# Cross attention on one core: which head VectorE scales in quads 8 to 15, one half of a layer norm a slot later, query copies moved, two weight sums swapped

## The chip, the core and the metric

The kernel runs on one core of one Trainium2 chip. The core has five engines with instruction queues of their own, each taken in order: TensorE (PE; its weight loads are listed as PEld), VectorE (DVE), ScalarE (ACT), GpSimd (POOL) and SyncE (SP), which issues the DMAs. The metric is the device time of one execution in microseconds. Before the change the median of three runs was 573.78 us (573.76 to 574.15).

## The reference

Eight batches of 256 tokens with 1024 features attend to 256 context vectors of the same batch. There are 32 heads of 32 features; the context serves as keys and as values without a projection. All is float32, and the mask is all ones.

```python
residual = hidden_states
x = (hidden_states - mu) * jax.lax.rsqrt(var + LN_EPS) * ln_gamma + ln_beta
Q = _split_heads(x @ Wq.T)
K = _split_heads(memory_keys)
V = _split_heads(memory_values)
scores = jnp.einsum('bhsd,bhtd->bhst', Q, K) * scale
probs = jax.nn.softmax(scores, axis=-1)
attn = jnp.einsum('bhst,bhtd->bhsd', probs, V)
out = attn.transpose(0, 2, 1, 3).reshape(B, S, HIDDEN) @ Wout.T
return residual + out
```

## The kernel before

**Quads and slots.** Four heads fill the 128 partitions, so a batch has 8 quads and the kernel 64, numbered 0 to 63; quads 8 to 15 are batch 1. The main loop (L934) has one slot for each n from 0 to 63. In slot n the kernel computes the scores of quad n + 1 (`scores`, L486), the weighted values of quad n - 2 (`values`, L633), some steps of the output projection of the batch before (`product_steps`, L717), query products for a batch to come (`make_q`, L345, or `query_product`, L447), and then the softmax of quad n + 1 (`softmax_parts`). The order of the calls is the order on each engine's queue; nothing reorders them. Both projections are done with seven block products in place of eight (Strassen's scheme in Winograd's form), from batch 2 on for the queries, so weights and operands have to be added and subtracted first; GpSimd does these sums.

**The softmax of one quad** goes head by head, j = 0 to 3, each head with 2 x 128 queries against 256 keys:
- `exps(j)`: VectorE adds the mask and takes the row minimum (L524), ScalarE takes the exponential and its row sum (L528).
- `normalize(j)`: VectorE takes the reciprocals of the sums, `rden` (L535), and an engine scales the head, two instructions of 128 x 256 (a pair, below). In quads 1 to 15 ScalarE scales head 3 (L538). The others are scaled by GpSimd (L543), except that in quads 10 to 15 VectorE scales head 2 (also L543).
- `blocks(j)`: VectorE transposes the head's 32 x 32 blocks (L549) into `pT`.
- `aside`: ScalarE copies half of that (L555) for two DMAs on SP's queue that move it between partitions.

The calls on quads 8 to 15 before the change run: `exps` 0, 1, 2, `normalize(0)`, `exps(3)`, hooks, `normalize(1)`, `blocks(0)`, hooks, `normalize(2)`, `normalize(3)`, `blocks(1)`, `aside(0)`, `blocks(2)`, query copies (quads above 8), `blocks(3)`, `aside(1)`. The hooks are evacuations of the output projection: `store` adds an accumulator in PSUM to the residual tile r on VectorE (L759) and sends it; `take` adds without sending (L755); `add_p1` adds a kept product to r on GpSimd (L750).

**Queries.** `copies` move query products from PSUM to the query tile `qa`: `copy_q` on ScalarE (L354), `copy_product` on ScalarE (L457) or VectorE (L468). In quads 0 to 8 they stand between `exps(3)` and `normalize(1)`; in later quads behind `blocks(2)`. A PSUM bank is free for TensorE's next product when its copy is done.

**The layer norm of a batch** is prepared slots ahead: loads, statistics on VectorE (L227, L230, L232), the power -1/2 on GpSimd (L235), then `ln_norm`: a small product on GpSimd (`shift`, L245) and one ScalarE instruction over a half of 128 x 1024 (L248). VectorE transposes its blocks (L316) and 16 DMAs move them (L332). For batch 2 the table has both halves' `ln_norm` in slot 3, the transpositions in slots 4 and 5, and the DMAs in slots 5 to 7. `ln_norm` is called in a slot after `softmax_parts`.

**Sums of weights.** `sum_wo` (L182) and `sum_wq` (L396) each write one chunk of 128 x 512 on GpSimd; a table gives the slot of each chunk. They are issued at the end of a slot, behind the sums of attention outputs (`sum_at`, L693), of x (`sum_x`, L435) and L235.

Of the kernel before, what the change touches and what calls it, by code (L numbers as in the profile page):

```python
# [59 lines left out]
def xattn_kernel(  # L60
# [10 lines left out]
    nc = tc.nc  # L71
# [4 lines left out]
    NQ = NC  # L76
    NH = P // HD
# [84 lines left out]
    B11, B21, B22, T1, T2, T3, T4 = range(7)  # L162
# [328 lines left out]
    def softmax(*args):  # L491
        for _ in softmax_parts(*args):
            pass

    tails = []
    BY_ACT = range(1, 2 * NQ)
    BY_DVE = range(NQ + 2, 2 * NQ)


    def softmax_parts(n, copies=(), ahead=(), between=(), hooks={}, fill=()):  # L500

        fill = list(fill)

        def fill_in():
            if fill:
                fill.pop(0)()  # L510

        pss = scs[n]
        pT = pTs[n] = ptp.tile([P, 2, NI, NH, NS, K], F32, tag="pT", name=f"pT_{n}")
        pc = asp.tile([P, NI, NH, NS, K], F32, tag="pc", name=f"pc_{n}")
        es, mns, dens = {}, {}, {}

        def exps(j, part=range(NS)):
            if 0 in part:
                es[j] = ep.tile([P, NS, T], F32, tag="e", name=f"e_{n}_{j}")
                mns[j] = sm.tile([P, NS], F32, tag="mn", name=f"mn_{n}_{j}")  # L520
                dens[j] = sm.tile([P, NS], F32, tag="den", name=f"den_{n}_{j}")
            e, mn, den = es[j], mns[j], dens[j]
            for s in part:
                nc.vector.tensor_tensor_reduce(  # L524
                    out=e[:, s, :], in0=pss[j][:, s, :], in1=mbs[n // NQ], scale=1.0,
                    scalar=NO_SCORE, op0=ALU.add, op1=ALU.min, accum_out=mn[:, s : s + 1],
                )
                nc.scalar.activation(  # L528
                    e[:, s, :], e[:, s, :], AF.Exp, bias=mn[:, s : s + 1], scale=-1.0,
                    accum_out=den[:, s : s + 1],  # L530
                )

        def normalize(j):
            rden = sm.tile([P, NS], F32, tag="rden", name=f"rden_{n}_{j}")
            nc.vector.reciprocal(rden, dens[j])  # L535
            for s in range(NS):
                if j == NH - 1 and n in BY_ACT:
                    nc.scalar.activation(  # L538
                        es[j][:, s, :], es[j][:, s, :], AF.Copy, scale=rden[:, s : s + 1]
                    )  # L540
                    continue
                engine = nc.vector if j == NH - 2 and n in BY_DVE else nc.gpsimd
                engine.tensor_scalar(  # L543
                    es[j][:, s, :], es[j][:, s, :], rden[:, s : s + 1], 1.0,
                    ALU.mult, ALU.mult,
                )

        def blocks(j):
            nc.vector.transpose(  # L549
                pT[:, :, :, j, :, :].rearrange("p a i s k -> p (a i) s k"),  # L550
                es[j].rearrange("p s (b t) -> p b s t", t=K),
            )

        def aside(j):
            nc.scalar.copy(pc[:, :, ts(j, 2)], pT[:, 1, :, ts(j, 2)])  # L555

        if n == 0:
            for j in range(NH - 1):
                exps(j, (0,))
            yield  # L560
            exps(NH - 1, (0,))
            fill_in()
            yield
            for j in range(NH):
                exps(j, (1,))
            normalize(0)
            fill_in()
        else:
            exps(0)
            while tails:  # L570
                tails.pop()()
            for done in list(pvs):
                copy_at(done)
            exps(1)
            for hook in hooks.get("soon", ()):
                hook()
            exps(2)
            normalize(0)
            exps(3)
        if n <= NQ:  # L580
            for copy in copies:
                copy()
        for hook in hooks.get(0, ()):
            hook()
        normalize(1)
        fill_in()
        blocks(0)
        for hook in hooks.get(1, ()):
            hook()
        normalize(2)  # L590
        fill_in()
        if n in BY_ACT:
            normalize(3)
        blocks(1)
        aside(0)
        if n not in BY_ACT:
            normalize(3)
        fill_in()
        blocks(2)
        while fill:  # L600
            fill_in()
        if n > NQ:
            for copy in copies:
                copy()

        def tail():
            blocks(3)
            aside(1)

            for r in range(2):  # L610
                nc.sync.dma_start(pT[ts(2 * r, K), 1], pT[ts(2 * r + 1, K), 0])
            for load in between:
                load()
            for r in range(2):
                nc.sync.dma_start(pT[ts(2 * r + 1, K), 0], pc[ts(2 * r, K)])

        for load in ahead:
            load()
        if n < NQ or n > N - NQ:
            tails.append(tail)  # L620
        else:
            tail()
        yield
# [16 lines left out]
    def copy_at(n):  # L640
        b, c = divmod(n, NQ)
        k, c = divmod(c, NK)
        if c == 0:
            ats[b, k] = atp.tile([P, NK, NS, NA, K], F32, tag="at", name=f"at_{b}_{k}")
        for r, pv in enumerate(pvs.pop(n)):
            nc.scalar.copy(  # L646
                ats[b, k][:, c, :, ts(r, 2), :], pv.rearrange("p a s k -> p s a k")
            )
# [148 lines left out]
    for n in range(N):  # L797
# [12 lines left out]
    loads, stats, norms, trans, moves, biases, masks = (  # L810
        {n: [] for n in range(N)} for _ in range(7)
    )
    for b in range(1, B):
        first = NQ * (b - 1) + 2
        if b == 1:
            when = dict(moves=())
        elif b == 2:
            when = dict(
                loads=(0, 1), stats=(2, 3), norms=(3, 3), trans=(4, 5),
                moves=tuple(5 + (i + 2) // 6 for i in range(16)),  # L820
            )
        else:
            when = dict(
                loads=(first - 12, first - 11) if b == SPLIT + 1 else (first - 13, first - 12),
                stats=(first - 10, first - 9) if b == SPLIT + 1 else (first - 11, first - 9),
                norms=(first - 8, first - 7), trans=(first - 7, first - 6),
                moves=tuple(first - 6 + (i + 2) // 6 for i in range(16)),
            )
        for table, key in (
            (loads, "loads"), (stats, "stats"), (norms, "norms"), (trans, "trans"),  # L830
        ):
            for i, n in enumerate(when.get(key, ())):
                assert n < first
                table[n].append((b, i))
        for n in range(N):
            part = [i for i, slot in enumerate(when["moves"]) if slot == n]
            if part:
                assert n < first - 1
                moves[n].append((b, part))
        biases[NQ * b - 2].append(b)  # L840
        if b % 2 == 0:
            masks[NQ * b - 7].append(b)
# [2 lines left out]
    sums = {n: [] for n in range(N)}  # L845
    for n, which, *chunks in (
        (0, T3, 0), (1, T3, 1), (2, T2, 0), (3, T2, 1), (4, T3, 2, 3), (5, T2, 2, 3),
        (6, T4, 0, 1), (9, T4, 2), (11, T4, 3),
    ):
        sums[n] += [partial(sum_wo, which, c) for c in chunks]  # L850
    for n, which, *chunks in (
        (6, "T1", 0), (7, "T1", 1, 2, 3), (8, "T2", 0, 1), (10, "T2", 2), (11, "T2", 3),
        (11, "T3", 0), (12, "T3", 1, 2), (13, "T3", 3), (13, "T4", 0), (14, "T4", 1, 2, 3),
    ):
        sums[n] += [partial(sum_wq, which, o) for o in chunks]
# [37 lines left out]
    for c in range(NC):  # L893
        copy_x0(1, c, nc.scalar if c < NC // 2 else nc.vector)
    first = softmax_parts(0, (partial(copy_q, 1), partial(copy_q, 2)), (), (), {}, [
        partial(ln_stats, 1, 0), partial(ln_stats, 1, 1),
        partial(ln_norm, 1, 0, nc.vector),
# [17 lines left out]
    for b in range(B - 1):  # L915
        done, ends = 0, b == B - 2
        for i, counts in enumerate(steps_of(b)):
            n = NQ * (b + 1) + i
# [238 lines left out]
```

## Time and profile before

| what | value |
|---|---|
| median of three runs | 573.78 us |
| the profiled execution | 573.95 us |
| its span, first to last instruction | 572.2 us |
| TensorE clock granted | 1.00 throughout |
| L543 on VectorE, quads 10 to 15 | 12 times, 10.1 us, one 0.34 to 1.46 us |
| L543 on GpSimd | 470 times, mean 0.478 us |
| L248 on ScalarE, batch 2 | 2 times, 2.37 us together |

Times in the profile are microseconds from the first instruction; lengths are of single instructions or, where a count stands behind "x", of a run of equal ones. An idle time in brackets is that of the engine just before the row, with the engine and the line whose end released it. Consecutive instructions of an engine overlap a little in their records (a transposition of 0.70 us is followed by the next after 0.61). Busy time of TensorE is modelled, so "busy" is not the same as "at its peak"; the lengths of equal slots tell more.

Slots 8 to 15, which hold the softmaxes of quads 9 to 16, lie between 81.78 us and 154.90 us of the span.

### The profile page before, as it was taken

The page shows a single profiled execution, that of the slowest core. Times are in us where ns is not written, and L with a number is a line of the kernel's source. Part 1 is how long each engine was busy: PE and PEld are TensorE (multiplying, and loading weights), DVE is VectorE, ACT ScalarE, POOL GpSimd, SP SyncE. Part 2 cuts the span into 40 slices and gives each one's busy share as a digit, 9 for nine tenths or more (in the row PEclk, how much of TensorE's full clock was granted, in tenths as well). Part 3 has the DMA queues.
Part 4 walks back from the last instruction along what each step waited for, and adds up shares of the span by engine and source line. Part 5 has one row for each costly group of instructions (what it writes and reads, how often), then busy time and mean ns, then how long its engine had stood idle before and what let it go on. Part 6 is the DMA issues. An engine that isn't in the chain of part 4 may idle for free.

```text
span 572.2 us, 20196 instructions
## 1 busy us (share of the span) xinstructions
PE 563.0 (98%) x7266; PEld 394.5 (69%) x7266; DVE 471.7 (82%) x1712; ACT 423.7 (74%) x1464; POOL 396.3 (69%) x640
## 2 busy tenths in 40 slices
PE   9999999899999999999999999999999999999997
PEld 8788786677567677677676677667766767755454
DVE  5889889899998888978888788988878768779823
ACT  4699998897678867688577867778767776869920
POOL 2788899798677674875568575677658667448780
PEclk9999999999999999999999999999999999999999
DMA  8966668754888666877788767986658865536751
GB/s 308 395 178 194 186 192 243 225 178 117 260 286 263 197 182 188 267 229 213 199 244 241 196 188 193 261 274 184 191 152 243 247 195 139 140 104 182 215 160 73
DMA packets 47219, 119.02 MB, mean 208 GB/s; under 512 B 8976, under 2 KB 9744, under 8 KB 47120
## 3 DMA queue, kind: packets, MB, share of 16 engines
q1 hardware_dynamic: 46976, 117.74, 69.0%
q8 instruction: 57, 0.93, 0.7%
q14 instruction: 42, 0.34, 0.2%
q10 hardware_dynamic: 144, 0.01, 0.0%
HBM read 66.33 MB, written 11.53 MB: 136 GB/s over the span
## 4 chain that ended last, share of the span: by engine, by line
PE 73%; DVE 8%; ACT 6%; POOL 6%; DMA 4%; issue 2%; SPq 0%; DVEq 0%; POOLq 0%; ACTq 0%
PE po_S L717 18%; PE pq_A L447 16%; PE pv L633 10%; PE po_A L717 9%; PE sc L486 9%; PE pq_S L447 6%; ACT e L528 4%; PE po_end L784 3%; DVE pT L549 2%; POOL e L543 2%; DVE e L524 2%; DMA x<-in_x_dram 2%; PE po_last L784 1%; DMA pT<-pT 1%; DVE e L543 1%
## 5 line engine op out<-in xcount | busy, mean ns | idle before, releaser
L543 POOL TENSOR_SCALAR e<-e,rden 128x256 f32<-128x256 f32 x470 | 216.8, 478 | 130.7 <-DVE rden L535 125.7
L528 ACT ACTIVATE e<-e,mn 128x256 f32<-128x256 f32 x512 | 254.0, 501 | 48.2 <-DVE mn L524 47.1
L549 DVE STREAM_TRANSPOSE pT<-e 128x512 f32<-128x512 f32 x256 | 179.0, 703 | 37.0 <-POOL e L543 28.6
L524 DVE CUSTOM_DVE_ANT_0 e<-sc,mb 128x256 f32<-128x256 f32 x512 | 185.2, 415 | 27.1 <-PE sc L486 26.8
L555 ACT COPY pc<-pT 128x512 f32<-128x512 f32 x128 | 78.9, 617 | 53.3 <-DVE pT L549 34.4
L528 ACT ACTIVATION_READ_ACCUMULATOR e<-e,mn 128x1 f32 x512 | 98.2, 192 | 0.0
L486 PEld LDWEIGHTS sc<-k,qa 32*128 32x128 f32 x1024 | 46.0, 184 | 43.5 <-issue 23.6
L486 PE MATMUL sc<-k,qa 32*128 32x256 f32 x1024 | 73.9, 401 | 1.0 <-DVE qa L468 0.9
L717 PE MATMUL po_S<-wo,at 128*128 128x512 f32 x152 | 74.4, 606 | 0.2 <-DVE r L759 0.2
L633 PE MATMUL pv<-pT,v 64*32 64x128 f32 x4096 | 74.1, 274 | 0.0
L633 PEld LDWEIGHTS pv<-pT,v 64*32 64x32 f32 x4096 | 57.0, 105 | 22.5 <-issue 12.8
L717 PE MATMUL po_A<-wo,at 128*128 128x512 f32 x128 | 59.4, 605 | 0.4 <-ACT qa L354 0.4
L345 PE MATMUL pq<-xnT,wq 128*128 128x256 f32 (+1 forms) x240 | 55.0, 383 | 0.6 <-ACT qa L354 0.6
L447 PEld LDWEIGHTS pq_A<-xnT,wq 128*128 128x128 f32 x416 | 48.5, 192 | 6.2 <-issue 5.3
L717 PE MATMUL po_S<-wo,s 128*128 128x512 f32 x104 | 50.3, 608 | 1.9 <-DVE r L759 1.8
L345 PEld LDWEIGHTS pq<-xnT,wq 128*128 128x128 f32 x240 | 44.6, 190 | 8.9 <-issue 1.5
L447 PE MATMUL pq_A<-xnT,wq 128*128 128x128 f32 x416 | 48.5, 275 | 0.0
L535 DVE RECIPROCAL rden<-den 128x2 f32<-128x2 f32 x256 | 38.1, 149 | 8.2 <-ACT e L528 7.1
L524 DVE DVE_READ_ACCUMULATOR2_ANT mn<- 128x1 f32 x512 | 42.2, 82 | 0.0
L717 PEld LDWEIGHTS po_A<-wo,at 128*128 128x128 f32 x128 | 22.9, 189 | 26.1 <-issue 24.5
L717 PEld LDWEIGHTS po_S<-wo,at 128*128 128x128 f32 x152 | 25.5, 190 | 19.9 <-issue 19.5
L646 ACT COPY at<-pv 128x128 f32<-128x128 f32 x128 | 26.1, 253 | 8.9 <-PE pv L633 8.9
(102 smaller groups left out, 676.1 us busy)
## 6 DMA issues: line engine op xcount, KB each, us to landing
v<-in_kv_dram SPq DMA_DIRECT2D x32, 512.0 KB, 4.3
pT<-pT SPq DMA_DIRECT2D x128, 128.0 KB, 2.6
pT<-pc SPq DMA_DIRECT2D x128, 128.0 KB, 4.2
ring<-kept_T SPq DMA_DIRECT2D x20, 512.0 KB, 5.1
k<-in_kv_dram SPq DMA_DIRECT2D x32, 256.0 KB, 3.6
x<-in_x_dram SPq DMA_DIRECT2D x15, 512.0 KB, 5.5
r<-in_x_dram SPq DMA_DIRECT2D x28, 256.0 KB, 5.1
out_dram<-r SPq DMA_DIRECT2D x28, 256.0 KB, 3.7
```

What stands on the lines that cost most here:

```text
L345: nc.tensor.matmul(pqs[n], wq[:, o, c, :], xnTs[b](c), start=(c == 0), stop=(c == NC - 1),)
L447: nc.tensor.matmul(pqs[b][:, o, :], w[:, c], x_[:, c], start=begins and o + c == 0, stop=c == NK - 1, skip_group_check=True,)
L486: nc.tensor.matmul(scs[n][j][:, s, :], qa[r, n % NQ, ts(s, P)], ks[n - n % 2][r, n % 2, :], start=True, stop=True,)
L524: nc.vector.tensor_tensor_reduce(out=e[:, s, :], in0=pss[j][:, s, :], in1=mbs[n // NQ], scale=1.0, scalar=NO_SCORE, op0=ALU.add, op1=ALU.m ...
L528: nc.scalar.activation(e[:, s, :], e[:, s, :], AF.Exp, bias=mn[:, s : s + 1], scale=-1.0, accum_out=den[:, s : s + 1],)
L535: nc.vector.reciprocal(rden, dens[j])
L543: engine.tensor_scalar(es[j][:, s, :], es[j][:, s, :], rden[:, s : s + 1], 1.0, ALU.mult, ALU.mult,)
L549: nc.vector.transpose(pT[:, :, :, j, :, :].rearrange("p a i s k -> p (a i) s k"), es[j].rearrange("p s (b t) -> p b s t", t=K),)
L555: nc.scalar.copy(pc[:, :, ts(j, 2)], pT[:, 1, :, ts(j, 2)])
L633: nc.tensor.matmul(pvs[n][r][j * HD : (j + 1) * HD], vs[n - n % 2][ts(r, 2 * K), i, ds(n % 2 * P + j * HD, HD)], pT[ts(r, 2 * K), :, i, j, ...
L646: nc.scalar.copy(ats[b, k][:, c, :, ts(r, 2), :], pv.rearrange("p a s k -> p s a k"))
L717: nc.tensor.matmul(po, operand(b, name)[:, c], wo[:, which, c], start=begins and c == 0, stop=c == NK - 1, skip_group_check=not begins,)
```

## The change

Four edits. In quads 8 to 15 (before: 10 to 15) VectorE scales head 1 (before: head 2), and GpSimd scales head 2; in these quads `normalize(2)` is called ahead of `blocks(0)`. Query copies of quad 9, whose softmax is in slot 8, stand between `exps(3)` and `normalize(1)`. The second half of batch 2's `ln_norm` is in slot 4. One chunk of `sum_wo` goes from slot 9 to slot 8, and one of `sum_wq` from slot 8 to slot 9.

```diff
-    BY_DVE = range(NQ + 2, 2 * NQ)
+    BY_DVE = range(NQ, 2 * NQ)
...
-                engine = nc.vector if j == NH - 2 and n in BY_DVE else nc.gpsimd
+                engine = nc.vector if j == 1 and n in BY_DVE else nc.gpsimd
...
-        if n <= NQ:
+        if n <= NQ + 1:
             for copy in copies:
                 copy()
         for hook in hooks.get(0, ()):
             hook()
         normalize(1)
         fill_in()
+        if n in BY_DVE:
+            normalize(2)
         blocks(0)
         for hook in hooks.get(1, ()):
             hook()
-        normalize(2)
+        if n not in BY_DVE:
+            normalize(2)
         fill_in()
...
-        if n > NQ:
+        if n > NQ + 1:
             for copy in copies:
                 copy()
...
-                loads=(0, 1), stats=(2, 3), norms=(3, 3), trans=(4, 5),
+                loads=(0, 1), stats=(2, 3), norms=(3, 4), trans=(4, 5),
...
-        (6, T4, 0, 1), (9, T4, 2), (11, T4, 3),
+        (6, T4, 0, 1), (8, T4, 2), (11, T4, 3),
...
-        (6, "T1", 0), (7, "T1", 1, 2, 3), (8, "T2", 0, 1), (10, "T2", 2), (11, "T2", 3),
+        (6, "T1", 0), (7, "T1", 1, 2, 3), (8, "T2", 0), (9, "T2", 1), (10, "T2", 2), (11, "T2", 3),
```

## The prediction

> **What bounds the kernel now.** I read the busy shares and the chain of waits first, then TensorE's timeline with its idle times, then the lengths of the loop's slots, then VectorE, GpSimd and ScalarE in the slots where TensorE stands still.
>
> ```profile
> PE 563.0 (98%) x7266; PEld 394.5 (69%) x7266; DVE 471.7 (82%) x1712; ACT 423.7 (74%) x1464; POOL 396.3 (69%) x640
> PE 73%; DVE 8%; ACT 6%; POOL 6%; DMA 4%; issue 2%; SPq 0%; DVEq 0%; POOLq 0%; ACTq 0%
> ```
>
> TensorE bounds the whole, but 27% of the chain is elsewhere. In order of time the chain is TensorE alone from 152.99 us on; before that it runs through the other engines. So only the start can pay. The TensorE timeline, start, length, and in brackets the idle time ahead:
>
> ```profile
> 61.36 2.83 PE L345 MATMUL pq<-xnT,wq 128*128 128x256 f32 x12 [0.63 <-ACT qa L354]
> 91.97 6.28 PE L717 MATMUL po_A<-wo,at 128*128 128x512 f32 x14 [0.41 <-ACT qa L354]
> 106.79 1.99 PE L717 MATMUL po_S<-wo,s 128*128 128x512 f32 x4 [1.75 <-DVE r L759]
> 138.00 3.81 PE L447 MATMUL pq_A<-sx,ring 128*128 128x128 f32 x32 [0.68 <-DVE qa L468]
> 146.36 0.71 PE L486 MATMUL sc<-k,qa 32*128 32x256 f32 x8 [0.95 <-DVE qa L468]
> 152.99 1.98 PE L717 MATMUL po_S<-wo,at 128*128 128x512 f32 x4 [0.18 <-DVE r L759]
> ```
>
> A slot (one value of n) begins with L486 on TensorE. Measured from one L486 to the next, slot 4 lasts 8.20 us (58.50 to 66.70) and slot 5, with the same work, 7.55. Slots 9 to 15 do what slots 17 to 23 do again without idle time: slot 9 lasts 8.84 against 8.37, slot 10 10.53 against 8.51, slots 11, 12 and 13 the same as their twins (9.37, 8.51, 8.51), slot 14 9.61 against 8.51, slot 15 10.20 against 8.51. The excess is 0.66, 0.47, 2.02, 1.10 and 1.69 us: 5.94 in all; behind 152.99 there is nothing to win.
>
> VectorE's scaling of the third head (L543) and GpSimd beside it:
>
> ```profile
> 96.69 2.73 DVE L543 TENSOR_SCALAR e<-e,rden 128x256 f32<-128x256 f32 x2
> 107.75 0.64 DVE L543 TENSOR_SCALAR e<-e,rden 128x256 f32<-128x256 f32 x2
> 116.09 0.63 DVE L543 TENSOR_SCALAR e<-e,rden 128x256 f32<-128x256 f32 x2
> 124.67 1.63 DVE L543 TENSOR_SCALAR e<-e,rden 128x256 f32<-128x256 f32 x2
> 133.33 2.67 DVE L543 TENSOR_SCALAR e<-e,rden 128x256 f32<-128x256 f32 x2
> 142.64 1.82 DVE L543 TENSOR_SCALAR e<-e,rden 128x256 f32<-128x256 f32 x2
> ...
> 94.94 1.83 POOL L543 TENSOR_SCALAR e<-e,rden 128x256 f32<-128x256 f32 x4
> 96.74 1.26 POOL L693 TENSOR_TENSOR s<-at,at 128x512 f32<-128x512 f32 x1
> ...
> 53.34 2.37 ACT L248 ACTIVATE x<-x,shift,rstd 128x1024 f32<-128x1024 f32 x2 [0.35 <-POOL shift L245]
> 60.39 0.82 ACT L354 ACTIVATE qa<-pq,qa 128x256 f32<-128x256 f32 x2
> ```
>
> One instruction, six times, 0.63 to 2.73 us for a pair. In quad 10 the first of the pair began at 96.69, GpSimd's sum L693 at 96.74, and both ended about together; so with the second and GpSimd's next sum. The short pairs met no large sum. The chain at that place:
>
> ```profile
> 100.64 2.30 issue
> 102.97 0.55 POOL rstd L235
> 103.52 1.25 POOL wo L182
> 104.78 1.23 POOL r L750
> ```
>
> GpSimd stands 2.3 us until VectorE, late by its scaling, delivers the variance (L232); then come L182 and L750, VectorE's store L759, and the 1.75 us of TensorE.
>
> **The change part by part.** Times are those of this execution; "lead" is how much earlier than before.
>
> **The norm a slot later.** ScalarE's two L248 take 1.14 each, at 53.34 to 55.62, ahead of quad 5's exponentials. Without the second, these start 1.14 earlier, and so do the query copies L354: done at 60.07, not 61.21. TensorE was ready for them at 60.66 (L633 from 59.57, 1.09 long): 0.66 won. The second L248 now stands behind slot 4's tail copy, which ended at 62.41, now 61.3; it ends at 62.45, before quad 6's exponentials began (62.69). Its shift (L245, 0.25) moves on GpSimd from slot 3 to slot 4, behind the scaling of head 2. That scaling started at 60.60 because of rden from ScalarE's exponentials; now about 59.3, so the sums behind start at 60.4, not 61.49: a GpSimd lead of 1.05. GpSimd is then the chain almost without a gap until 75.70, so VectorE and ScalarE keep about 1.05. The block transposition of that half (slot 5, at 65.73) and its DMAs on SP's queue stay behind the same instructions. Were that cover gone, the L248 would cost its 1.14.
>
> **Quads 8 and 9.** Two more scaling pairs on VectorE, one GpSimd pair (0.93) less each. A pair alone is 0.63; it now comes right behind rden of head 1, when GpSimd scales head 0. The row for that: at 142.64 the first of a pair took 0.55 against 0.35, beside a GpSimd scaling that began at 142.56. So 0.63 to 1.03 a pair; I take 0.85, the middle. Quad 8 hides it: VectorE stood 0.26 and 0.78 us there. Quad 9 does not (no idle time from 87.60 to 91.75): VectorE's lead falls to 0.2.
>
> The Trainium skill, page "SBUF — State Buffer", section "Who interferes with whom", speaks against this place: any GpSimd instruction holds the port pair shared with VectorE whole, and VectorE's two-port scaling then blocks fully. The sums above agree. By the rule each scaling could wait a GpSimd scaling's 0.48, a pair 1.6, and eight pairs would be up to 6 us dearer than by 0.85.
>
> **Query copies of slot 8.** Two L354 of 0.36 move in front of the fourth head's scaling and one tail copy. Ready with the exponentials (before 89.43, lead 1.05), they end at 89.1; TensorE is ready at 91.49 - 0.66 = 90.8, so 0.47 is won. The scaling behind them waits for rden until 89.4 anyway; without that it would be 0.7 later.
>
> **Quads 10 to 15.** The order does the work: GpSimd's second pair now waits for rden of head 2, which VectorE computes behind its own scaling. Between head 0 and head 2 GpSimd can start no sum. VectorE can meet a sum only when GpSimd is still at the slot before; then rden of head 2 and the transposition of head 0 queue behind the pair, and GpSimd's second pair waits for that rden.
>
> Slots 9 and 10: VectorE starts quad 10 at 91.5, scales at 94.6 to 95.5 beside head 0, transposes until 98.4 (before 101.23), delivers L232 at 99.95 (102.81). GpSimd: head 2 from 95.8, done 96.75; three sums of 1.25 to 100.6; rstd 0.55; one sum, then L750 until 103.6 (106.01). L759 ends 104.3. TensorE arrives there at 97.04 + 1.07 + 1.09 + 0.96 + 3.57 = 103.73: 0.62 us idle stay, 1.40 of 2.02 are won.
>
> Slots 11 to 13: TensorE full, lead 2.53, so slot 14 begins at 132.6. The others must hold it. ScalarE (8.25 us of work in slots 10 and 11) has a lead of 2.6 from VectorE's and keeps it. In quad 12 nothing changes. In quad 13 GpSimd ends its sums at 120.85, VectorE comes at 121.0 and pays about 1.0, not 1.63. In quad 14 VectorE comes at 128.85, GpSimd's last sum ends at 129.3: about 1.15 instead of 2.67. L468 ends at 132.95 (before 137.85); TensorE needs it at 134.8. GpSimd's last sum into the ring ends at 135.15, needed at 137.5. All 1.10 of slot 14 are won.
>
> Slots 14 and 15: quad 15's scores now come at 133.7 and hold VectorE. It scales at 137.3, waits for a sum until 137.65, L468 ends at 141.35; the second half of slot 15's scores is due at 141.08 + 0.54 = 141.6. Then mask bias, exponentials, L759 at 148.2; TensorE is there at 147.8. Of 1.69, 1.27 are won. GpSimd is the thin place: its sums take 6.25 us in slots 11 to 13, its scaling 1.85, and the hold about 0.9: 9.0 a slot against TensorE's 8.51, paid from the lead.
>
> **The swapped sums.** L182 and L396 take 1.25 each; slots 8 and 9 keep theirs. Their readers are products of slots 13 and 14. Nothing, within 0.05.
>
> Sum: 0.66 + 0.47 + 1.40 + 1.10 + 1.27 = 4.90. Span 572.2 - 4.9 = 567.3. The execution took 573.95, 1.75 around its span, and the median of three is 573.78: 573.78 - 4.9 = **568.9**. From slot 16 on TensorE has no idle time and the code is the same.
>
> **The rivals.**
> All idle time goes (0.62 and 0.42 too): 573.78 - 5.94 = 567.8. For it: these rests hang on L759 alone. Against: GpSimd's row of sums up to L750 has no gap to give.
> The scalings of quads 13 to 15 still meet sums, because GpSimd, held between its heads, falls behind: slots 14 and 15 keep their excess. 573.78 - 0.66 - 0.47 - 1.40 = 571.25. For it: 9.0 against 8.51. Against: the lead of 2.5.
> L750 comes no earlier: only ScalarE's two edits pay, 573.78 - 1.13 = 572.65. For it: the sums are as many as before. Against: the 2.3 us that GpSimd stood for L232.
> Slower: GpSimd falls behind for good. It decides from where GpSimd's last sum ends over 1.25 us after VectorE's rden of head 1; then every pair of quads 10 to 15 costs 2.7. 6 x 2.7 + 2 x 0.85 - 10.1 = 7.8 more for VectorE; less 1.45 idle in quad 12 and the 1.13 of ScalarE, 5.2: 579.0. For it: the hold. Against: GpSimd began head 0 late only in quad 10, by 0.12 us; in quad 12 it stood 1.94 before it, in quad 15 1.08.
> That the change doesn't do what it says is hardly one: the loop calls the scaling directly behind rden of head 1 in all eight quads, and VectorE takes its queue in order.
>
> **How the numbers follow.** The forecast (568.0 to 570.3, from the pair at 0.63 or 1.03 and one sum met in quad 14 or 15) 0.58; all idle gone 0.10; half of it 0.17; ScalarE alone 0.06; slower 0.09. A difference under 0.2%, 1.15 us, can't be told from none: the ScalarE case is at that bound and counts as same. Faster 0.85, same 0.06, slower 0.09. The range 567.7 to 571.6 holds the first three and leaves out 0.2.
>
> **What would show it.** VectorE's L543 sixteen times, mostly 0.34 to 0.6 us, not 0.95. TensorE's waits for L354 gone; at L759 in slot 10 0.6 instead of 1.75; at L468 none. GpSimd's L543 466 times, not 470, and GpSimd waiting for rden ahead of its second pair. Slot 16 begins near 150.0, not 154.9. Wrong would be: long pairs in quads 13 to 15, or a new wait of TensorE for the ring.

## The result, and the profile after

The changed kernel took 570.98 us (median, 570.41 to 571.32); the kernel before, beside it on the same chip, 573.94. The ratio is 0.9947 with a 95% interval of 0.993 to 0.9965: faster by 2.96 us, where 4.90 was forecast (568.9). The profiled execution took 571.32 us, its span 569.5. The added code has three lines, so L717, L750, L759, L693 and L633 of before are now L720, L753, L762, L696 and L636; kernels below that leave those lines out keep the old numbers. The medians below are over all executions; three far longer ones (637 us of e_copies, 1366 of a_late2 and 1979 of the kernel before) are left out of the ratios.

The page's busy shares and chain of waits of the changed kernel:

```profile
PE 561.8 (99%) x7266; PEld 393.9 (69%) x7266; DVE 468.5 (82%) x1716; ACT 423.7 (74%) x1464; POOL 394.0 (69%) x636
PE 80%; POOL 7%; DVE 5%; ACT 3%; issue 3%; DMA 1%; SPq 0%; DVEq 0%; POOLq 0%; ACTq 0%
```

TensorE's share of the chain rises from 73% to 80%, not to the whole: 20% is still elsewhere. TensorE's timeline shows where, with the only two rows between 56 and 160 us that have an idle time (in brackets):

```profile
105.56 1.98 PE L720 MATMUL po_S<-wo,s 128*128 128x512 f32 x4 [1.20 <-DVE r L762]
...
145.91 1.13 PE L720 MATMUL po_S<-wo,s 128*128 128x512 f32 x2 [1.31 <-POOL wo L182]
```

The waits for L354 in two slots, for L468, and the 0.18 us for the store in slot 15 are gone. The wait for the store in slot 10 is 1.20 us, not the 0.62 of the forecast. The second row is new: TensorE waits for a weight sum of GpSimd. Slot lengths, from one L486 to the next, in us (the slot from 58.50 us, which the prediction calls slot 4, is slot 5 by the count of the others; only slots that differ are shown):

| slot | before | after | without idle time |
|---|---|---|---|
| 5 | 8.20 | 7.55 | 7.55 |
| 9 | 8.84 | 8.36 | 8.37 |
| 10 | 10.53 | 9.98 | 8.51 |
| 14 | 9.61 | 8.51 | 8.51 |
| 15 | 10.20 | 9.89 | 8.51 |

Won: 0.65, 0.48, 0.55, 1.10 and 0.31, together 3.09. Left: 1.47 in slot 10 and 1.38 in slot 15.

VectorE's scaling L543 in the changed kernel, from VectorE's timeline, all eight quads:

```profile
81.12 0.62 DVE L543 TENSOR_SCALAR e<-e,rden 128x256 f32<-128x256 f32 x2
88.03 0.61 DVE L543 TENSOR_SCALAR e<-e,rden 128x256 f32<-128x256 f32 x2
95.84 1.04 DVE L543 TENSOR_SCALAR e<-e,rden 128x256 f32<-128x256 f32 x2
105.62 0.62 DVE L543 TENSOR_SCALAR e<-e,rden 128x256 f32<-128x256 f32 x2
113.72 0.62 DVE L543 TENSOR_SCALAR e<-e,rden 128x256 f32<-128x256 f32 x2
122.29 0.90 DVE L543 TENSOR_SCALAR e<-e,rden 128x256 f32<-128x256 f32 x2
130.09 1.09 DVE L543 TENSOR_SCALAR e<-e,rden 128x256 f32<-128x256 f32 x2
138.64 1.05 DVE L543 TENSOR_SCALAR e<-e,rden 128x256 f32<-128x256 f32 x2
```

Eight pairs take 6.55 us; the six of before took 10.12. None of them lasts as long as one that met a large sum before (1.63 to 2.73). What GpSimd does around a pair, for the one at 113.72 (heads 0 and 2 of its quad, no sum between them):

```profile
112.44 0.93 POOL L543 TENSOR_SCALAR e<-e,rden 128x256 f32<-128x256 f32 x2 [1.16 <-DVE rden L535]
114.73 0.93 POOL L543 TENSOR_SCALAR e<-e,rden 128x256 f32<-128x256 f32 x2 [1.35 <-DVE rden L535]
```

GpSimd's timeline has the three rows that the rest of the case turns on:

```profile
67.92 0.93 POOL L543 TENSOR_SCALAR e<-e,rden 128x256 f32<-128x256 f32 x2 [0.64 <-DVE rden L535]
...
91.53 0.55 POOL L235 TENSOR_TENSOR rstd<-ve,mhalf 128x1 f32<-128x1 f32 x1 [1.19 <-DVE ve L232]
...
144.58 1.28 POOL L182 TENSOR_TENSOR wo<-wo 128x512 f32<-128x512 f32 x1
```

In the first GpSimd stands for a reciprocal; in the second for the variance of slot 8; the third is the sum that TensorE waits for in slot 15. To compare executions I count from the L486 near 58.5 us (58.50 before, 58.92 after). GpSimd's L235 in slot 8 then comes at 32.20 us before and at 32.61 after: 0.41 later, though the norm edit was to bring it earlier. From there the chain runs through GpSimd's sums without a gap that could give, in the chain of waits of the changed kernel:

```profile
99.22 1.24 POOL sx L435
...
102.31 1.24 POOL wq L396
103.55 1.25 POOL r L753
104.82 0.70 DVE r L762
105.56 1.98 PE po_S L720 x4
```

### The profile page after: what moved, and what is told of

It is laid out like the page before. It is cut to its first block, busy times and chain, and to the rows that moved or that the text cites. A ratio compares the mean times of both kernels' runs of the same rounds, so it can differ in the third digit from the quotient of the medians.

```text
span 569.5 us, 20200 instructions
## 1 busy us (share of the span) xinstructions
PE 561.8 (99%) x7266; PEld 393.9 (69%) x7266; DVE 468.5 (82%) x1716; ACT 423.7 (74%) x1464; POOL 394.0 (69%) x636
## 4 chain that ended last, share of the span: by engine, by line
PE 80%; POOL 7%; DVE 5%; ACT 3%; issue 3%; DMA 1%; SPq 0%; DVEq 0%; POOLq 0%; ACTq 0%
PE po_S L720 20%; PE pq_A L447 18%; PE pv L636 10%; PE sc L486 10%; PE po_A L720 10%; PE pq_S L447 7%; PE po_end L787 3%; ACT e L528 2%; POOL e L543 2%; DVE e L524 2%; DVE pT L549 1%; PE po_last L787 1%; POOL wq L396 1%; POOL wo L182 1%; DMA pT<-pT 1%
## 5 line engine op out<-in xcount | busy, mean ns | idle before, releaser
L543 POOL TENSOR_SCALAR e<-e,rden 128x256 f32<-128x256 f32 x466 | 215.3, 478 | 128.7 <-DVE rden L535 126.1
L549 DVE STREAM_TRANSPOSE pT<-e 128x512 f32<-128x512 f32 x256 | 179.0, 704 | 35.6 <-POOL e L543 26.2
L486 PEld LDWEIGHTS sc<-k,qa 32*128 32x128 f32 x1024 | 46.2, 184 | 42.1 <-issue 20.1
L720 PE MATMUL po_S<-wo,at 128*128 128x512 f32 x152 | 74.3, 606 | 0.0
L636 PE MATMUL pv<-pT,v 64*32 64x128 f32 x4096 | 74.1, 274 | 0.0
L486 PE MATMUL sc<-k,qa 32*128 32x256 f32 x1024 | 73.6, 401 | 0.1
L636 PEld LDWEIGHTS pv<-pT,v 64*32 64x32 f32 x4096 | 57.0, 105 | 22.5 <-issue 12.4
L720 PE MATMUL po_A<-wo,at 128*128 128x512 f32 x128 | 59.4, 605 | 0.0
L720 PE MATMUL po_S<-wo,s 128*128 128x512 f32 x104 | 50.2, 607 | 2.5 <-POOL wo L182 1.3
L720 PEld LDWEIGHTS po_A<-wo,at 128*128 128x128 f32 x128 | 23.0, 190 | 25.6 <-issue 24.4
L720 PEld LDWEIGHTS po_S<-wo,at 128*128 128x128 f32 x152 | 25.5, 190 | 19.5 <-issue 19.5
L753 POOL TENSOR_TENSOR r<-r,p 128x512 f32<-128x512 f32 x24 | 30.6, 1275 | 5.0 <-DMA r<-in_x_dram 4.0
```

The source lines that it names most:

```text
L486: nc.tensor.matmul(scs[n][j][:, s, :], qa[r, n % NQ, ts(s, P)], ks[n - n % 2][r, n % 2, :], start=True, stop=True,)
L543: engine.tensor_scalar(es[j][:, s, :], es[j][:, s, :], rden[:, s : s + 1], 1.0, ALU.mult, ALU.mult,)
L549: nc.vector.transpose(pT[:, :, :, j, :, :].rearrange("p a i s k -> p (a i) s k"), es[j].rearrange("p s (b t) -> p b s t", t=K),)
L636: nc.tensor.matmul(pvs[n][r][j * HD : (j + 1) * HD], vs[n - n % 2][ts(r, 2 * K), i, ds(n % 2 * P + j * HD, HD)], pT[ts(r, 2 * K), :, i, j, ...
L720: nc.tensor.matmul(po, operand(b, name)[:, c], wo[:, which, c], start=begins and c == 0, stop=c == NK - 1, skip_group_check=not begins,)
L753: nc.gpsimd.tensor_tensor(r, r, p1s[b], ALU.add)
```

## The experiments

Two sets: parts of the change alone on the kernel before, and then single mends or reversals on the changed kernel. Times are medians; each ratio is to the kernel before, run beside it on the same chip. Beside these kernels the kernel before took 575.08, 574.83 and 574.60 us in the mean of each set of runs, and 573.95 beside the changed kernel, in part because some of its executions had a lower TensorE clock (last section). So for the same time the ratios here come out up to 0.002 lower than the first one, and what decides below are the traces.

**The two ScalarE edits, each alone.**

```diff
 e_norm:
-                loads=(0, 1), stats=(2, 3), norms=(3, 3), trans=(4, 5),
+                loads=(0, 1), stats=(2, 3), norms=(3, 4), trans=(4, 5),
 e_copies:
-        if n <= NQ:
+        if n <= NQ + 1:
...
-        if n > NQ:
+        if n > NQ + 1:
```

> The kernel before with the norm edit alone. Theory: ScalarE's edit wins TensorE 0.66 us in slot 4, but slot 10's wait for L759 ends when GpSimd and VectorE get there, and their lead fell to about 0.2 us by slot 6 in the changed kernel; the 0.66 turns up as a longer wait in slot 10, so the time is 0.0 to 0.3 us shorter (573.5 to 573.9). Rival (the sum on record): the terms add, 0.66 us shorter (573.2).

> The kernel before with slot 8's query copies moved, alone. Theory: slot 9 loses its 0.47 us of idle time and slot 10's wait grows by as much: no change, 573.7 to 574.0. Rival: the terms add, 0.47 us shorter (573.4).

Measured: the norm edit 574.12 us, ratio 0.999 (0.9973 to 1.0007); the copies 574.88, ratio 1.0001 (0.9987 to 1.0014). Neither is told from no change. The waits of TensorE that grew, first with the norm edit, then with the copies:

```profile
92.26 6.28 PE L717 MATMUL po_A<-wo,at 128*128 128x512 f32 x14 [0.93 <-ACT qa L354]
```

```profile
106.77 3.36 PE L717 MATMUL po_S<-wo,s 128*128 128x512 f32 x4 [2.29 <-DVE r L759]
```

The norm edit takes 0.67 out of slot 5 (7.53 us) and slot 9's wait grows from 0.41 to 0.93; what TensorE won it stands later, most of it already in slot 9 and not, as expected, in slot 10. The copies take 0.47 out of slot 9 and the wait in slot 10 grows from 1.75 to 2.29, by 0.54. In both, the later wait ends at a time that the edit hardly moves: 33.31 us after the L486 near 58.5 against 33.47 before, and 48.36 against 48.29. With the copies alone the four products behind the wait also took 3.36 us, not 1.99 (last section), and slot 14 lasted 8.86 us, not 9.61.

**The scaling alone**, in all eight quads, and in the six that VectorE had before.

```diff
 both:
-                engine = nc.vector if j == NH - 2 and n in BY_DVE else nc.gpsimd
+                engine = nc.vector if j == 1 and n in BY_DVE else nc.gpsimd
...
+        if n in BY_DVE:
+            normalize(2)
         blocks(0)
...
-        normalize(2)
+        if n not in BY_DVE:
+            normalize(2)
 e_scale only:
-    BY_DVE = range(NQ + 2, 2 * NQ)
+    BY_DVE = range(NQ, 2 * NQ)
```

> The kernel before with the scaling edit alone (head 1 on VectorE in quads 8 to 15, the second reciprocal and GpSimd's pair ahead of the first transposition). Theory: it alone sets when L759 ends in slot 10 and when GpSimd ends its sums in slot 14, so it wins nearly all that the whole change wins: 570.9 to 571.3, with slot 4's and slot 9's idle times back and slot 10's wait shorter by about as much. Rival: the terms add, so 1.1 us of the gain is missing: 572.1.

> As the run before, but only in quads 10 to 15. Theory: without the pair of quad 9 VectorE delivers the variance (L232) of slot 8 0.6 to 0.7 us earlier, GpSimd starts its row of sums up to L750 as much earlier, and both of TensorE's remaining waits (L759 in slot 10, the sum L182 in slot 15) are 0.6 us shorter: 570.2 to 570.7. Rival: the two quads relieve GpSimd of a pair each, and without that it is later: 571.5 to 572.5. Second rival: they don't matter, the same as the run before.

Measured: 571.18 us, ratio 0.9936 (0.9919 to 0.9953), and 570.80, ratio 0.9925 (0.9907 to 0.9944). The scaling edit alone gives what the whole change gives, and its two added quads give nothing. The theory for six quads failed in its mechanism: slot 10 has no wait in either kernel; the wait that is shorter without the two quads is slot 9's (0.41 against 1.03), and slot 15's goes only from 1.35 to 1.24. TensorE's waits with the scaling in all eight quads:

```profile
61.54 5.42 PE L345 MATMUL pq<-xnT,wq 128*128 128x256 f32 x24 [0.64 <-ACT qa L354]
...
92.77 6.28 PE L720 MATMUL po_A<-wo,at 128*128 128x512 f32 x14 [1.03 <-ACT qa L354]
...
145.95 1.12 PE L720 MATMUL po_S<-wo,s 128*128 128x512 f32 x2 [1.35 <-POOL wo L182]
```

Here the two waits for ScalarE stand, and the wait in slot 10 isn't there at all. In the changed kernel it is the other way round. The store in slot 10 (L759, now L762) starts 47.54 us after the mark before, 46.16 with the scaling alone, 45.90 after: the scaling moves it by 1.4, the ScalarE edits by 0.26. What these win ahead of it, TensorE loses again at it.

**Which head.** The whole change, but VectorE scales the third head as before.

```diff
-                engine = nc.vector if j == 1 and n in BY_DVE else nc.gpsimd
+                engine = nc.vector if j == NH - 2 and n in BY_DVE else nc.gpsimd
...
-        if n in BY_DVE:
-            normalize(2)
         blocks(0)
...
-        if n not in BY_DVE:
-            normalize(2)
+        normalize(2)
```

> The changed kernel with VectorE scaling head 2 again, in the old order of calls, but still in quads 8 to 15; the other three edits stay. Theory: VectorE meets GpSimd's sums again (a pair 1.6 to 2.7 us in most quads) and the gain is gone: 573.0 to 575.5. Rival: the gain comes from relieving GpSimd of two pairs and from ScalarE's edits, not from which head it is: 571 to 572.

Measured: 577.97 us, ratio 1.0053 (1.0034 to 1.0073), slower than I had expected. Two of its pairs on VectorE, and what TensorE waits for:

```profile
81.81 2.74 DVE L543 TENSOR_SCALAR e<-e,rden 128x256 f32<-128x256 f32 x2
...
99.10 2.73 DVE L543 TENSOR_SCALAR e<-e,rden 128x256 f32<-128x256 f32 x2
```

```profile
109.18 3.47 PE L717 MATMUL po_S<-wo,s 128*128 128x512 f32 x4 [3.60 <-DVE r L759]
```

Quad 8's pair now meets GpSimd's three sums into the tile `ring` (L396, one run of 3.83 us from 81.85) and the variance of slot 8 is late by that; GpSimd stands 2.51 us for it; quad 10's pair meets sums as before the change. So the gain needs the head or the order of calls that goes with it, both of which this run puts back, and with the third head and the old order more quads on VectorE are a loss. Part of the loss is a lower clock behind the stop of 3.60 us (last section).

**Short pairs, or an early reciprocal?** In the changed kernel VectorE computes head 2's reciprocal ahead of the transposition of head 0. This run puts the call behind it and leaves the head that VectorE scales.

```diff
-        if n in BY_DVE:
-            normalize(2)
         blocks(0)
         for hook in hooks.get(1, ()):
             hook()
-        if n not in BY_DVE:
-            normalize(2)
+        normalize(2)
```

> The changed kernel, but the reciprocal and the scaling of head 2 are called behind the transposition of head 0 in quads 8 to 15; VectorE still scales the second head. Theory (what counts is that the pair lies where GpSimd runs no sum; the place of the next reciprocal only holds GpSimd longer): pairs of 0.6 to 1.1 us, GpSimd some 0.6 us later with its sums, slots 10 and 15 longer by 0.3 to 0.6 each, 571.5 to 572.2. Rival (the reciprocal's place ahead of the transposition is what wins the time): GpSimd so late that pairs meet sums again, over 573.

Measured: 574.99 us, ratio 1.0008 (0.9995 to 1.0021). The whole gain is gone, which is the rival's time, but not by the rival's mechanism. The pairs stay short (0.61 to 1.38 us, none met a whole sum); it is GpSimd that is late. Its timeline, the scaling of head 2 in quads 13, 14 and 15:

```profile
124.99 0.94 POOL L543 TENSOR_SCALAR e<-e,rden 128x256 f32<-128x256 f32 x2 [0.96 <-DVE rden L535]
...
133.98 0.94 POOL L543 TENSOR_SCALAR e<-e,rden 128x256 f32<-128x256 f32 x2 [0.89 <-DVE rden L535]
...
143.04 0.94 POOL L543 TENSOR_SCALAR e<-e,rden 128x256 f32<-128x256 f32 x2 [0.96 <-DVE rden L535]
```

In the changed kernel the same three stops are 0.38, none and 0.38. The difference, 0.58 + 0.89 + 0.58, is 2.05 us, on top of 0.7 that GpSimd was behind by the store of slot 10 (46.57 us after the mark against 45.90) and 0.4 from the stops of quads 11 and 12. The weight sum L182 that slot 15 needs then ends 3.2 later (90.18 us after the mark against 86.94). Slot 10 lasts 10.63 us, and TensorE waits in slot 15 twice:

```profile
145.36 0.71 PE L486 MATMUL sc<-k,qa 32*128 32x256 f32 x8 [1.56 <-DVE qa L468]
149.01 1.13 PE L717 MATMUL po_S<-wo,s 128*128 128x512 f32 x2 [1.83 <-POOL wo L182]
```

So short pairs alone win nothing here; the reciprocal that lets GpSimd go on is needed too. What that reciprocal would win with the third head on VectorE no run shows, because a_head2 puts both back.

**One mend each, on the changed kernel.** Quads 8 and 9 back to GpSimd (a_q10); the transposition of batch 2's x, L316, behind the scaling of head 2 (a_fill); the last chunk of the weight sums T1 ahead of slot 14's other sums (a_t1).

```diff
 a_q10:
-    BY_DVE = range(NQ, 2 * NQ)
+    BY_DVE = range(NQ + 2, 2 * NQ)
 a_fill, ahead of the call of softmax:
+            if trans[n]:
+                fill.insert(0, lambda: None)
 a_t1:
-        sums[n] += [partial(sum_wo, T1, c) for c in chunks]
+        sums[n][:0] = [partial(sum_wo, T1, c) for c in chunks] if n == 14 else []
+        sums[n] += [partial(sum_wo, T1, c) for c in chunks] if n != 14 else []
```

> The changed kernel with VectorE's scaling in quads 10 to 15 only. Theory: VectorE's pair in quad 9 delays L232, and with it GpSimd's row of sums up to L750: without it the wait in slot 10 falls from 1.20 to about 0.5, and the one in slot 15 by about 0.6: 0.6 to 0.8 us shorter than the changed kernel (570.2 to 570.4). Rival: GpSimd, with a pair more in quads 8 and 9, is later: 0.5 us longer (571.5).

> The changed kernel; in slots 4 and 5 the transposition of x (L316) stands behind the reciprocal of head 2, not ahead of it. Theory: GpSimd's lead from the norm edit (0.8 us behind slot 4) was lost in slot 5, where its pair for head 2 waited 0.64 us for a reciprocal behind L316; kept, it makes L759 in slot 10 and the sums of slot 14 about 0.5 us earlier: 570.3 to 570.6. Rival: the lead is lost elsewhere before slot 8: 571.0, no change.

> The changed kernel; in slot 14 GpSimd does the chunk of L182 ahead of its three L396, not behind them. Theory: TensorE's 1.31 us wait in slot 15 is for this sum alone; L759 in slot 15 ends 148.2 and is needed at 149.1, so nothing takes the wait's place: 1.2 to 1.4 us shorter than the changed kernel (569.6 to 569.8). Rival: the wait passes to L759 or to a weight chunk of L396 that now comes 1.25 us later: under 0.5 us shorter (570.5 to 571.0).

Measured: 570.24 us, ratio 0.9909 (0.9889 to 0.993); 570.13, ratio 0.9907 (0.9886 to 0.9928); 569.43, ratio 0.990 (0.9877 to 0.9922). The first two act on slot 10. TensorE's wait there is 0.66 and 0.47 in place of 1.20, in that order of kernels:

```profile
104.23 1.98 PE L720 MATMUL po_S<-wo,s 128*128 128x512 f32 x4 [0.66 <-DVE r L762]
```

```profile
104.28 1.98 PE L720 MATMUL po_S<-wo,s 128*128 128x512 f32 x4 [0.47 <-DVE r L762]
```

L235 in slot 8 comes at 32.06 and 31.87 us from the mark, 0.55 and 0.74 earlier than in the changed kernel, and the wait shrinks by 0.54 and 0.73. That settles both causes. Neither helps slot 15, whose wait is 1.34 in both (1.31 in the changed kernel): the chunk moves earlier with GpSimd, and TensorE arrives earlier by as much. In a_t1 slot 15 lasts 8.51 and slot 10 still waits 1.22.

**All three mends together, and then without the ScalarE edits.** The second kernel is the first with the norm and copies edits undone.

> The changed kernel with three mends at once: the transposition of x behind the scaling of the quad, quads 8 and 9 scaled as before the change, and the last chunk of T1 summed ahead of slot 14's other sums. Theory (the two waits that are left in slots 10 and 15 have one cause each, and both are named): slots 10 and 15 both last 8.51 us, 1.47 and 1.38 less than in the changed kernel, 2.85 together; about 568.1. Rival (the first and the second mend give the same time in slot 10, or the store by L759 takes the place of the chunk in slot 15): one of the two slots keeps 0.4 us or more, 568.6 to 569.2.

> The run before it, with the norm back in slot 3 and the query copies of slot 8 back behind the scaling. Theory (these two edits gave nothing alone because the time turned up again in slot 10's wait; where no such wait is left it stays won): 0.66 + 0.47 longer than the run before it, about 569.2. Rival (they are worth nothing here either, because slot 10 waits longer or shorter by as much): the same as the run before it, within 0.3.

Measured: 568.45 us (567.84 to 570.93), ratio 0.9904 (0.9886 to 0.9922), and 568.78 (568.70 to 568.93), ratio 0.9903 (0.9888 to 0.9919). The first is the fastest version found, by the median. The intervals of both lie below that of the changed kernel (0.993 to 0.9965) and, beside the same runs of the kernel before, below that of the changed kernel with the sums swapped back (0.9929 to 0.9958, below). With all three mends the page's chain of waits is TensorE's nearly alone:

```profile
PE 97%; DVE 1%; DMA 1%; POOL 0%; ACT 0%; issue 0%; POOLq 0%
```

There is no idle time ahead of any TensorE row between 56 and 160 us; slots 10 and 15 last 8.58 and 8.50. Of the 5.94 us excess of before 5.78 are won: from the start of slot 5 to that of slot 16 it is 90.62 us, 96.40 before. The store of slot 10 ends 45.26 us after the mark and the product behind it begins at 45.34, so it is just in time. Without the ScalarE edits one wait comes back:

```profile
61.47 5.42 PE L345 MATMUL pq<-xnT,wq 128*128 128x256 f32 x24 [0.65 <-ACT qa L354]
```

That is the norm's 0.65 in slot 5. The copies' 0.47 in slot 9 is not there (8.37 us): the mends have brought quad 9's exponentials early enough (the last ends 30.27 us after the mark, 31.03 before). So the expected 1.13 for both edits was half right in the trace: slots 5 to 15 together are 0.58 longer. In the medians the difference is 0.33, within the spread of the first kernel.

**The swapped sums**, back in their old order.

```diff
-        (6, T4, 0, 1), (8, T4, 2), (11, T4, 3),
+        (6, T4, 0, 1), (9, T4, 2), (11, T4, 3),
...
-        (6, "T1", 0), (7, "T1", 1, 2, 3), (8, "T2", 0), (9, "T2", 1), (10, "T2", 2), (11, "T2", 3),
+        (6, "T1", 0), (7, "T1", 1, 2, 3), (8, "T2", 0, 1), (10, "T2", 2), (11, "T2", 3),
```

> The changed kernel with the two sums of slots 8 and 9 in their old order. Theory: nothing, 570.8 to 571.2. Rival (slot 9's later sum delays the store by L759 or a product that reads the chunk): over 0.5 us either way.

Measured: 570.95 us, ratio 0.9944 (0.9929 to 0.9958), as the changed kernel; slots 10 and 15 last 9.99 and 9.87.

## Why the prediction was right, and where not

Right: the direction, the engine, and the reason. VectorE's pairs are short because GpSimd runs no sum between head 0 and head 2, and the waits for L468 in slot 14 vanish (1.10 forecast, 1.10 measured). The price of a pair held: 0.85 x 8 = 6.8 us forecast, 6.55 measured, 0.61 or 0.62 where no scaling or sum of GpSimd lies beside it, or only the last 0.2 us of one, and 0.90 to 1.09 where more does. The rule of the Trainium skill that was weighed there (page "SBUF — State Buffer", section "Who interferes with whom": whoever issues first has the shared ports for the whole instruction) would have made a pair up to 1.6, by the prediction's estimate; the changed kernel shows at most 0.47 above a pair alone there, so 1.09. The longest at this place in another run is 1.38 (a_late2), beside the end of a sum. Beside GpSimd's sums it holds in kind: 2.73 and 2.74. The swapped sums are worth nothing, as said.

The time itself owes something to luck. 570.98 lies outside the 568.0 to 570.3 that the prediction gives for its own mechanism, next to a rival (571.25) in which quads 13 to 15 still meet sums and slots 14 and 15 keep their excess. The trace excludes that rival: these pairs are short and slot 14's excess is gone; what stayed lies in slots 10 and 15 and has the causes below.

Wrong, by its own steps:

1. "VectorE and ScalarE keep about 1.05" behind the norm edit. GpSimd's lead was 0.81 at 61.10 us and 0.18 at 75.88 (16.96 us from the mark against 17.14). The rows are, first before and then in the changed kernel:

```profile
61.49 1.90 POOL L366 TENSOR_TENSOR wq<-wq,gs 128x1024 f32<-128x1024 f32 x1
75.64 2.56 POOL L182 TENSOR_TENSOR wo<-wo 128x512 f32<-128x512 f32 x2
...
61.10 1.89 POOL L366 TENSOR_TENSOR wq<-wq,gs 128x1024 f32<-128x1024 f32 x1
75.88 2.55 POOL L182 TENSOR_TENSOR wo<-wo 128x512 f32<-128x512 f32 x2
```

The 0.63 between them is the new stop of 0.64 at 67.92, in quad 6. The prediction's own numbers held the reason: the moved L248 ends at 62.45, quad 6's exponentials began at 62.69, so ScalarE's lead from there is 0.24 and not 1.05. It measured 0.25 (62.86 - 58.92 against 62.69 - 58.50). "Ends before its reader began" makes an edit free, but it doesn't keep the lead of what stands behind. The other half is VectorE's order, in the changed kernel's timeline:

```profile
65.81 0.17 DVE L535 RECIPROCAL rden<-den 128x2 f32<-128x2 f32 x1 [0.76 <-ACT e L528]
65.89 1.23 DVE L316 STREAM_TRANSPOSE xe<-x 128x1024 f32<-128x1024 f32 x1
67.04 0.67 DVE L549 STREAM_TRANSPOSE pT<-e 128x512 f32<-128x512 f32 x1
67.63 0.31 DVE L535 RECIPROCAL rden<-den 128x2 f32<-128x2 f32 x2
```

The reciprocal that GpSimd waits for stands behind L316 and L549, in quad 5 as in quad 6. In quad 5 GpSimd's stop there, 0.85 us, is the same before and after; with L316 out of the way (a_fill) it is gone, L235 in slot 8 comes 0.74 earlier and the store of slot 10 0.72.

2. "VectorE's lead falls to 0.2" at quad 9: it fell below nothing. L235 came 0.41 later than before. The pairs of quads 8 and 9 cost that path 0.55 (a_q10), 0.63 between the two kernels with the scaling alone; the runs don't part quad 8's share from quad 9's.

3. Slot 10, "1.40 of 2.02 are won": 0.55. The store came 47.54 - 45.90 = 1.64 earlier; but TensorE also came earlier, by 0.65 + 0.48 of the slots before. 1.64 - 1.13 = 0.51. The terms 0.66 and 0.47 were won where it was said; the sum's third term was mis-sized by 0.85, and steps 1 and 2 (0.74 and 0.55) are more than that. Because of them the two ScalarE edits were worth little, 0.2 us by the medians (570.98 against 571.18 for the scaling alone) and 0.3 by the slots: without them TensorE meets nearly the same store without a wait.

4. Slot 15, "1.27 are won": 0.31. The store that was named there was no longer late. What took its place is the sum L182 for a chunk of T1, the last in GpSimd's row of slot 14. Before, its row began at 146.77 and lasted 1.28, and TensorE went on at 148.11, so it ended just under the waits that were removed:

```profile
146.77 1.28 POOL L182 TENSOR_TENSOR wo<-wo 128x512 f32<-128x512 f32 x1
...
148.11 1.12 PE L717 MATMUL po_S<-wo,s 128*128 128x512 f32 x2
```

The prediction looked up when GpSimd's last sum into the ring is due, and named a new wait for the ring as a sign of being wrong; when this sum, into `wo`, is due it did not look up. It lies at the end of the row that the prediction called the thin place. One line of the table (a_t1) takes it away.

The time lies inside the range because the steps that failed cost less than half of the excess: 2.85 of 5.94 remained. The forecast of a start of slot 16 near 150.0 us became 154.90 - 3.06 + 0.42 = 152.26 in the span's time, where 0.42 is how much later the mark lies.

Two slips carry nothing: the mean of one scaling on VectorE before was 0.88 us, not 0.95 (0.45 after), and the chances outside the range add up to 0.15, not 0.2.

## What to carry to other kernels

Waits on one path don't add: time won ahead of a wait whose end doesn't move is stood there, so sum the releases along each engine's own chain and take the later one at each meeting point. When a wait goes, list what else that engine's next instructions need and when it ends, above all transfers and sums that now end just under the old wait. Where two engines share a resource, look at what a reordering lets the other one start: here the short instruction without the early reciprocal won nothing (a_late2).

## What the runs showed of the hardware

In the traces a stop of TensorE of 2.29 us, and one of 3.60, went with a stretch at half the clock; stops of 1.75 us at the same place (before) and of 1.83 us (a_late2, slot 15) did not. The stretches of the kernel with the copies alone (window, sum, busy time of PE, PEld, DVE, ACT and POOL, granted clock, DMA share, GB/s); the stop lasts from 104.48 to 106.77:

```profile
104.00:106.00 2.00, 0.48 (x5) 0.29 (x3) 1.69 (x11) 2.00 (x9) 2.00 (x3) 1.00 0.90 229
106.00:108.00 2.00, 1.23 (x2) 0.64 (x3) 1.79 (x5) 1.68 (x8) 2.00 (x5) 0.81 1.06 374
108.00:110.00 2.00, 2.00 (x3) 0.34 (x1) 2.00 (x6) 1.52 (x4) 2.00 (x3) 0.50 1.00 368
110.00:112.00 2.00, 2.00 (x61) 1.51 (x65) 0.75 (x4) 2.00 (x6) 1.97 (x2) 0.84 0.05 18
```

In windows of 0.5 us the clock is 0.73 from 107.0, 0.50 in the next six windows and 0.86 from 110.5. If it takes only the values one and one half, it was halved from 107.23 to 110.64, for 3.41 us, and the fall came 0.46 us after the work had begun again. With the third head it is 0.80 from 108.5, 0.50 in the next six windows and 0.79 from 112.0: halved from 108.80 to 112.21, again 3.41 us, but here it fell 0.38 us ahead of the end of the stop (109.18). It cost 1.4 and 1.5 us on the four products (3.36 and 3.47 against 1.98).

The Trainium skill, page "TensorE: Matmul & The Clock Gate", section "What's actually happening", gives a free-running window of 3.4 us, which agrees with the length of the slow stretch; its half clock "after ≥1 idle window" doesn't follow from a stop of 2.29 us, which is shorter than a window.

The length of the stop doesn't seem to decide alone. Of the 23 executions of the kernel before that ran beside the copies, nine have a mean clock of 0.996 or 0.997, about what one such stretch gives (1.7 us lost in 573), and took 575.9 to 576.5 us; five executions of the kernel with the copies have 1.000. No trace of these was kept, so where their clock fell, and what decides, no run shows. A wait that grows can cost more than itself.
